# A four-layer convolution and attention network: sign convolutions with two weights packed in one float32r number, attention without a row-maximum pass

## The chip, the cores and the metric

The kernel runs on one core of a Trainium2 chip. The core has a matrix engine (TensorE, PE in the profile), a vector engine (DVE), a scalar engine (ACT), a general one (GpSimd, POOL) and a queue engine (SyncE, SP) that issues transfers. Each has its own program; they wait for each other through semaphores. TensorE writes to an accumulator memory (PSUM[...]) that DVE and ACT read. The metric is device time in microseconds (us), the median of several runs; the spans and times of single instructions come from a hardware profile of one execution, whose span is a few us longer.

## The reference, cut to what matters

The input is 16 images of 256 channels and 28 x 28 pixels. Each of the four layers keeps that shape.

```python
# layer 0: binary convolution, batch norm, residual
y  = conv3x3(sign(x), sign(w0)) * mean_abs(w0)
x1 = batchnorm(y) + x

# layer 1: sign convolution with float weights, two gated branches
res = prelu(x1, a_alpha1)
y = prelu(bn(conv3x3(sign(x1 + a_move), clip(a_w)), a_bn1), a_alpha2)
y = se_gate(s*x1 + (1-s)*y) * y * res          # gate: means, two small matrices, sigmoid
y = bn(y, a_bn2) + res
u = prelu(bn(conv1x1(sign(y + f_move), clip(f_w)), f_bn1), f_alpha2)
u = se_gate(s2*y + (1-s2)*u) * u
x2 = bn(u, f_bn2) + y

# layer 2: two binary convolutions; the batch norms use the batch's statistics
o = prelu(binconv(sign(batchnorm(x2)), w1), a1)
o = prelu(binconv(sign(batchnorm(o)), w2), a2)
x3 = prelu(batchnorm(o) + x2, a3)

# layer 3: attention over the 784 pixels of each image, 64 channels
q, k, v = Wq x3, Wk x3, Wv x3
out = Wp (softmax(q^T k / 8) v) + x3
```

A batch norm with the batch's own statistics needs all 16 images before any can go on, so there are barriers after layer 0, layer 1 and each convolution of layer 2.

## The kernel before

Channels lie on the 128 partitions (two halves), pixels on the free axis. Signs and sign weights are bfloat16. The float weights of layer 1 are split into three bfloat16 parts whose sum is exact, so each of its products is done three times.

```python
def conv3x3(ps, pad, wts, mo):          # called with [w0], w1 (three parts), [w2a], [w2b]
    n, last = 0, len(wts) * 18 - 1
    for w in wts:
        for k in range(2):
            for t in range(9):
                r, c = divmod(t, 3)
                for h in range(2):
                    T.matmul(               # line 145
                        ps[:, h, :HN].rearrange("p (a b) -> p a b", b=S),
                        lhsT=w[:, k, t, mo * P:(mo + 1) * P],
                        rhs=pad[:, k, r + h * HR:r + h * HR + HR, c:c + S],
                        start=(n == 0), stop=(n == last),
                    )
                n += 1
# ...
def conv2(b, w, alpha):                 # layer 2
    for mo in range(2):
        ps = conv_ps()                  # three tiles of two banks
        conv3x3(ps, pads[b % 2], [w], mo)
        p = prelu_n(ph, ps[:, :, :HN], alpha[:, mo:mo + 1])
        A.copy(halves(nt[b][:, mo, :]), ps[:, :, :HN])
        for h in range(2):
            V.bn_stats(stats[:, mo, 2 * b + h, :], p[:, h, :])
```

The attention computes the scores twice: once to find each row's maximum, and once, transposed, with the maximum subtracted through a 65th row of q and k.

```python
def row_max(b):
    # ...
    for c in range(NC_):                # 7 chunks of 112 rows
        ps = two_banks(pssc, "sc")
        for h in range(2):
            T.matmul(ps[:MC, h, :HN], lhsT=q[0:64, c * MC:(c + 1) * MC],
                     rhs=k_[0:64, h * HN:(h + 1) * HN], start=True, stop=True)      # line 543
        V.tensor_reduce(nm[:, c:c + 1], ps[:MC, :, :HN], AX.XY, ALU.max, negate=True)
# ...
def attend(b):
    # ...
    def scores(c):
        ps = two_banks(pssc, "sc")
        for h in range(2):
            T.matmul(ps[:MC, h, :HN], lhsT=k_[:, c * MC:(c + 1) * MC],
                     rhs=q[:, h * HN:(h + 1) * HN], start=True, stop=True)          # line 569
        es[c] = ph.tile([MC, 2, HN], F32, tag="es", name="es", bufs=3)
        A.activation(es[c], ps[:MC, :, :HN], AF.Exp, scale=0.125)
    # ...
            for h in range(2):
                T.matmul(av[:, h, :HN], lhsT=v_[:, c, :], rhs=es[c][:, h, :],
                         start=(c == 0), stop=(c == NC_ - 1))                       # line 581
    V.reciprocal(r, av[64:P, :, :HN])   # columns 64.. of v are ones: the denominators
    V.tensor_tensor(o, av[0:64, :, :HN], r, ALU.mult)
# ...
for b in range(B):
    nm = row_max(b)
    if pending is not None:
        project(*pending)
    if b + 1 < B:
        qkv(b + 1)
    put_max(b, nm)
    if b + 2 < B:
        finish2(b + 2)
    pending = (b, attend(b))
```

Here P = 128, N = 784, HN = 392 (half an image, one PSUM bank), HR = 14, S = 28, MC = 112, NC_ = 7. V, A, T are the vector, scalar and matrix engine. All 16 images' x2 and integers stay in SBUF.

Of the kernel before, what the change touches and what calls it, by code (L numbers as in the profile page):

```python
"""conv_seq d4 on 16x256x28x28: binary conv + BN, two-branch SE block, binary conv x2 + BN, attention.

Layout: channels on partitions (two halves of 128), pixels (784) on the free axis, one tile per
image.  Activations that are signs (-1, 0, 1) and sign weights are held in bfloat16, and
convolution sums of signs (integers of magnitude <= 2304) in int16: both hold them exactly.  The
float32 weights that meet sign activations (layer 1) are split into three bfloat16 parts whose sum
is the float32 weight, so that these products are exact too; everything else is float32.

Algebra used: stop_gradient(a - b) + b is a; sums of 2304 signs never reach the saturation of layer
0; the mean of s*x + (1-s)*y is taken from the two means; a per-channel constant of layer 1's output  # L10
is carried along (`cc`) into layer 2's last bias, as layer 2's first batch norm doesn't see it.
"""
# [10 lines left out]
BF = mybir.dt.bfloat16  # L23
I16 = mybir.dt.int16
AF = mybir.ActivationFunctionType
ALU = mybir.AluOpType
AX = mybir.AxisListType
PSUM = bass.MemoryType.PSUM

P = 128  # L30
B = 16
S = 28
N = S * S          # pixels of an image
HN = N // 2        # half an image: one matmul, one PSUM bank
HR = S // 2
K9 = 256 * 9
MC = 112           # attention rows per chunk
# [3 lines left out]
#: The per-channel vectors, in the order of their columns.  # L41
# [10 lines left out]
def conv_seq_kernel(ctx: ExitStack, tc: tile.TileContext, d: dict, out: bass.AP):  # L52
# [6 lines left out]
    xr = ctx.enter_context(tc.tile_pool(name="xr", bufs=B))  # L59

# [9 lines left out]

    pads = [const.tile([P, 2, S + 2, S + 2], BF, tag=f"pad{i}", name=f"pad{i}") for i in range(2)]
    for p in pads:
        nc.gpsimd.memset(p, 0.0)

# [7 lines left out]
    def inv_std(name, var):  # L82
        """1 / sqrt(var + EPS) of a [P, 2] tile, the square root's table corrected by a Newton step."""
# [9 lines left out]
    def affine(name, inv, gamma, beta, mean):  # L93
        """scale = gamma * inv and bias = beta - mean * scale."""
        s, c = vtile(name + "_s"), vtile(name + "_c")
        tt(s, gamma, inv, ALU.mult)
        tt(c, mean, s, ALU.mult)
        tt(c, beta, c, ALU.subtract)
        return s, c

# [1 line left out]
    def load_taps(pool, src, k, g):  # L102
        st = pool.tile([P, 3, 256], F32, tag="st", name="st", bufs=2)
# [3 lines left out]
    def sign_chunk(pool, dst, src, acc, k, g):  # L107
        """Three taps of sign(w) into dst, and their part of sum |w| in PSUM, [P, 2]."""
        st = load_taps(pool, src, k, g)
        A.activation(dst[:, k, 3 * g:3 * g + 3, :], st, AF.Sign)  # L110
        ab = pool.tile([P, 256], F32, tag="ab", name="ab", bufs=2)
        V.tensor_reduce(ab, st.rearrange("p t o -> p o t"), AX.X, ALU.add, apply_absolute_value=True)
        part = acc.tile([P, 2], F32, tag="sm", name="sumabs")
        for mo in range(2):
            T.matmul(part[:, mo:mo + 1], lhsT=ab[:, mo * P:(mo + 1) * P], rhs=ones, start=True, stop=True)
        return part

    def sign_weights(pool, dst, src, total, acc):
# [35 lines left out]
    def inner(pad, k):  # L154
        return pad[:, k, 1:S + 1, 1:S + 1]
# [517 lines left out]
```

## Time and profile before

The time is 2254.1 us, the median of three runs from 2253.57 to 2255.21. The profile's span is 2262.4 us.

| stretch of the span | us | PE busy | DVE busy | ACT busy | granted PE clock |
|---|---|---|---|---|---|
| opening, weights of layer 0 | 0 to 22.6 | 14.5 | 11.1 | 10.6 | 1.00 |
| layer 0 | 22.6 to 217 | 187.4 | 57.2 | 66.8 | 0.99 |
| layer 1 | 217 to 911 | 681.3 | 317.4 | 139.9 | 0.99 |
| layer 1's last images, barrier | 911 to 929 | 5.4 | 11.9 | 5.6 | 0.69 |
| layer 2, first convolution | 929 to 1131 | 199.4 | 100.7 | 61.4 | 0.98 |
| barrier | 1131 to 1143 | 0.9 | 9.6 | 2.3 | 0.73 |
| layer 2, second convolution | 1143 to 1345 | 198.2 | 139.4 | 57.9 | 0.99 |
| barrier, first images of attention | 1345 to 1490 | 124.0 | 90.9 | 29.9 | 0.66 |
| one image of attention | 1541 to 1592 | 47.5 | 36.9 | 12.1 | 0.80 |
| eight images of attention | 1648 to 2089 | 413.8 | 143.3 | 64.1 | 0.74 |
| the last of attention | 2089 to 2262 | 154.1 | 49.2 | 21.4 | 0.70 |

Busy times are sums over the instructions of an engine in the stretch. Matmuls are pipelined and their ends are modelled, so a busy PE need not work at its peak; the time from one start to the next is the better measure. The granted clock is the share of full speed that the hardware gave TensorE. A float32 matmul appears as two records, each with a weight load of its own. In a line of a group, the name after the engine is the operation, then output<-inputs, shapes, type and count; after the bar come the busy time in us and the mean of one in ns, and then the engine's idle time before the group and what ended it.

### The profile page before, as it was taken

How to read it: one execution, taken by the hardware profiler on the slowest of the kernel's cores; microseconds unless marked ns; L12 is line 12 of the kernel's file. 1: busy time of each engine (PE TensorE's matmuls, PEld its weight loads, DVE VectorE, ACT ScalarE, POOL GpSimd, SP SyncE). 2: the span in 40 equal slices, each digit the busy share in tenths (PEclk: the TensorE clock that was granted, in tenths of full speed). 3: DMA queues.
4: the chain of work that ended last, by engine and by line, in shares of the span. 5: the costliest groups of instructions: out<-in, count | busy, mean ns of one | idle time of the engine just before them, and what ended most of it. 6: DMA issues, size and time to landing. Idle time of an engine off the chain costs nothing.

```text
span 2262.4 us, 22710 instructions
## 1 busy us (share of the span) xinstructions
PE 2126.3 (94%) x9896; PEld 1170.4 (52%) x9896; DVE 1041.2 (46%) x1628; ACT 496.2 (22%) x659; POOL 6.5 (0%) x13
## 2 busy tenths in 40 slices
PE   8998999999999998699989979999999999999997
PEld 4554555555555555355545544444444444444443
DVE  5213244454454454554567765677653233222232
ACT  5322122122122111323222321222211111111111
POOL 0000000000000000000000000000000000000000
PEclk9999999999999999799999985688778777777776
DMA  5221000000000000100000000000000000000000
GB/s 204 73 72 43 1 29 29 15 29 15 15 29 15 15 15 1 42 1 1 1 1 1 1 5 1 14 14 15 14 14 15 14 15 14 14 14 14 15 15 28
DMA packets 11603, 50.11 MB, mean 22 GB/s; under 512 B 1776, under 2 KB 2160, under 8 KB 11504
## 3 DMA queue, kind: packets, MB, share of 16 engines
q1 hardware_dynamic: 11504, 48.67, 6.2%
q8 instruction: 77, 1.26, 0.2%
q14 instruction: 22, 0.18, 0.0%
HBM read 35.82 MB, written 12.85 MB: 22 GB/s over the span
## 4 chain that ended last, share of the span: by engine, by line
PE 90%; DVE 8%; ACT 1%; issue 0%; DMA 0%; SPq 0%; ACTq 0%
PE cv L145 53%; PE sc L543 10%; PE sc L569 7%; PE av L581 6%; PE mi L594 4%; DVE r L586 4%; PE cv L372 3%; PE mi L522 3%; PE mi L531 2%; PE av L554 2%; PE gate L343 1%; DVE nm L547 1%; DVE p L187 1%; DVE x L515 0%; DVE t L186 0%; DVE x L511 0%
## 5 line engine op out<-in xcount | busy, mean ns | idle before, releaser
L145 PE MATMUL cv<-pad,w 128*128 128x392 bf16 x4608 | 799.4, 333 | 8.7 <-ACT pad L305 8.7
L145 PEld LDWEIGHTS <-w 128*128 128x128 bf16 x4608 | 445.0, 97 | 343.6 <-issue 12.2
L543 PE MATMUL sc<-qk 64*112 64x392 f32 x448 | 263.8, 764 | 51.6 <-DVE nm L547 51.6
L543 PEld LDWEIGHTS sc<-qk 64*112 64x112 f32 x448 | 116.3, 267 | 186.9 <-issue 116.9
L145 PE MATMUL cv<-pad,w2b 128*128 128x392 bf16 x1152 | 198.3, 334 | 11.1 <-ACT pad L465 11.1
L569 PE MATMUL sc<-qk 65*112 65x392 f32 x448 | 202.8, 575 | 0.0
L145 PE MATMUL cv<-pad,w2a 128*128 128x392 bf16 x1152 | 198.3, 333 | 2.4 <-ACT pad L436 2.4
L294 DVE TENSOR_SCALAR t<-sy,vec 128x784 f32<-128x784 f32 x32 | 20.1, 628 | 340.7 <-ACT sy L318 340.7
L581 PE MATMUL av<-es,va 112*128 112x392 f32 x448 | 170.2, 509 | 1.6 <-ACT es L574 1.6
L586 DVE RECIPROCAL r<-av 64x784 f32<-64x784 f32 x16 | 80.9, 5057 | 190.3 <-PE av L581 190.3
L547 DVE TENSOR_REDUCE nm<-sc 112x1 f32<-112x784 f32 x112 | 108.9, 972 | 121.2 <-PE sc L543 120.8
L145 PEld LDWEIGHTS <-w2b 128*128 128x128 bf16 x1152 | 111.9, 97 | 97.5 <-issue 13.6
L145 PEld LDWEIGHTS <-w2a 128*128 128x128 bf16 x1152 | 112.2, 98 | 87.3 <-issue 3.9
L186 DVE TENSOR_SCALAR t<-cv,vec 128x784 f32<-128x784 f32 x64 | 66.2, 1034 | 158.6 <-PE cv L145 158.6
L574 ACT ACTIVATE es<-sc 112x784 f32<-112x784 f32 x112 | 91.9, 823 | 205.3 <-PE sc L569 205.2
L569 PEld LDWEIGHTS sc<-qk 65*112 65x112 f32 x448 | 85.7, 202 | 82.9 <-issue 71.5
L581 PEld LDWEIGHTS av<-es,va 112*128 112x128 f32 x448 | 87.7, 196 | 69.4 <-issue 18.7
L446 ACT CAST n<-cv 128x784 int16<-128x784 f32 x64 | 52.0, 812 | 229.3 <-DVE p L187 229.3
L318 ACT ACTIVATE sy<-cv,abn_c,abn_s 128x784 f32<-128x784 f32 x32 | 32.1, 1003 | 315.4 <-PE cv L145 315.4
L594 PE MATMUL mi<-o,wp 64*128 64x392 f32 x128 | 88.3, 831 | 7.2 <-DVE o L587 6.2
L246 DVE BATCH_NORM_STATS2 stats<-cv 128x6 f32<-128x392 f32 x64 | 33.4, 564 | 125.8 <-ACT y L244 125.7
L522 PE MATMUL mi<-x,wqk 128*128 128x392 f32 x128 | 68.0, 688 | 14.3 <-DVE x L515 14.3
(182 smaller groups left out, 1536.9 us busy)
## 6 DMA issues: line engine op xcount, KB each, us to landing
xs<-in_x_dram SPq DMA_DIRECT2D x32, 784.0 KB, 4.3
out_dram<-x SPq DMA_DIRECT2D x16, 784.0 KB, 3.3
st<-in_w_dram SPq DMA_DIRECT2D x12, 384.0 KB, 3.9
st<-in_w2a_dram SPq DMA_DIRECT2D x6, 384.0 KB, 3.1
st<-in_w2b_dram SPq DMA_DIRECT2D x6, 384.0 KB, 3.2
stf<-in_fw_dram SPq DMA_DIRECT2D x1, 256.0 KB, 2.8
wqk<-in_wqk_dram SPq DMA_DIRECT2D x1, 128.0 KB, 2.1
wv<-in_wv_dram SPq DMA_DIRECT2D x1, 64.0 KB, 1.9
```

Of the source, the lines that this page charges most:

```text
L145: T.matmul(ps[:, h, :HN].rearrange("p (a b) -> p a b", b=S), lhsT=w[:, k, t, mo * P:(mo + 1) * P], rhs=pad[:, k, r + h * HR:r + h * HR + H ...
L186: V.tensor_scalar(t, n, 0.0, alpha, ALU.min, ALU.mult)
L372: T.matmul(ps[:, h, :HN], lhsT=w[:, k, mo * P:(mo + 1) * P], rhs=z2[b][:, k, h * HN:(h + 1) * HN], start=(n == 0), stop=(n == 5),)
L446: A.copy(halves(nt[b][:, mo, :]), ps[:, :, :HN])
L522: T.matmul(ps[:, h, :HN], lhsT=wqk[:, k, :], rhs=x2[b][:, k, h * HN:(h + 1) * HN], start=(k == 0), stop=(k == 1),)
L543: T.matmul(ps[:MC, h, :HN], lhsT=q[0:64, c * MC:(c + 1) * MC], rhs=k_[0:64, h * HN:(h + 1) * HN], start=True, stop=True,)
L547: V.tensor_reduce(nm[:, c:c + 1], ps[:MC, :, :HN], AX.XY, ALU.max, negate=True)
L569: T.matmul(ps[:MC, h, :HN], lhsT=k_[:, c * MC:(c + 1) * MC], rhs=q[:, h * HN:(h + 1) * HN], start=True, stop=True,)
L574: A.activation(es[c], ps[:MC, :, :HN], AF.Exp, scale=0.125)
L581: T.matmul(av[:, h, :HN], lhsT=v_[:, c, :], rhs=es[c][:, h, :], start=(c == 0), stop=(c == NC_ - 1))
L586: V.reciprocal(r, av[64:P, :, :HN])
L594: T.matmul(ps[:, h, :HN], lhsT=wp[:, mo * P:(mo + 1) * P], rhs=o[:, h, :], start=True, stop=True)
```

## The change

**Sign convolutions.** A sum of at most 2304 signs is a small integer. The change puts the weights of two output channels into one float32r number, a + 4095 b (a for the first half of the channels, b for the second), and convolves once for both. ACT rounds the sum divided by 4095 to the integer part (adding and DVE then taking away 1.5 x 2^23), and two more matmuls with scaled unit matrices separate the halves: -4095 times the rounded value is added to the first half's sum, and the value itself goes to the second. To stay in range, only 15 of the 18 taps are packed; the last three are done for each half by itself.

```diff
+            sg = pool.tile([P, 3, 256], BF16, tag="t1", name="sg", bufs=2)
+            A.activation(sg, st, AF.Sign, saturate=False)
+            V.scalar_tensor_tensor(dst[0][:, n], sg[:, :, P:], PACK, sg[:, :, 0:P], ALU.mult, ALU.add)
 ...
+    def sign_conv(pss, pad, w, temp):
 ...
+        for h in range(2):
+            for n in range(5):
+                for t in range(3):
+                    product(pss[0], h, w[0][:, n, t, :], n, t, n + t == 0, n + t == 6)
+            r, bs[h] = temp("t1"), temp("up", FR)
+            A.activation(r, pss[0][:, h, :HN], AF.Identity, bias=rounding, scale=1.0 / PACK)
+            V.tensor_scalar(bs[h], r, -ROUND, None, ALU.add)
+        for h in range(2):
+            for mo in range(2):
+                for t in range(3):
+                    product(pss[mo], h, w[1][:, t, mo * P:(mo + 1) * P], 5, t, mo == 1 and t == 0, False, mo == 0)
+        for h in range(2):
+            for mo in range(2):
+                T.matmul(
+                    pss[mo][:, h, :HN], lhsT=unpack[mo], rhs=bs[h], start=False, stop=True,
+                    skip_group_check=(mo == 0),
+                )
```

**Layer 1.** The float weights are split into two float32r parts instead of three bfloat16 ones. Two output rows are computed from four combinations of the padded rows (a minimal-filtering transform: four products in place of six), which DVE forms in float32r. The parametric ReLU is done as x + (1 - alpha) * relu(-x), its ReLU on ACT. The two gates' small matmuls are joined. Integers and x2 go to DRAM and come back.

```diff
+            terms = (
+                (e0, e1, ALU.subtract), (o0, e1, ALU.add), (e1, o0, ALU.subtract), (o0, o1, ALU.subtract)
+            )
+            for pair in ((1, 2), (0, 3)):
+                for k in range(2) if b == 0 else (slice(0, 2),):
+                    for u in pair:
+                        x, y, op = terms[u]
+                        tt(vs[b % 2][:, u, k], x[:, k], y[:, k], op)
 ...
+        def conv(b, mo, u, ps):
+            n = 0
+            for k in range(2):
+                for w in w1:
+                    for c in range(3):
+                        T.matmul(
+                            ps.rearrange("p (a b) -> p a b", b=S),
+                            lhsT=w[:, k, c, u, mo * P:(mo + 1) * P],
+                            rhs=vs[b % 2][:, u, k, :, c:c + S],
+                            start=(n == 0), stop=(n == 11),
+                        )
+                        n += 1
 ...
+            A.activation(t1, ps[:, 0, :HN], AF.Identity, bias=c1[:, mo:mo + 1], scale=s1[:, mo:mo + 1])
+            V.scalar_tensor_tensor(up, ps[:, 1, :HN], s1[:, mo:mo + 1], t1, ALU.mult, ALU.add)
+            V.scalar_tensor_tensor(vp, ps[:, 1, :HN], ns1[:, mo:mo + 1], t1, ALU.mult, ALU.add)
 ...
+            nc.gpsimd.dma_start(out=x2d[b], in_=x2[b])
```

At the barriers a batch of matmuls on unused data is put on TensorE, to keep its clock from falling.

```diff
+        def keep_busy(v, n):
+            A.copy(idle[:, 0:2], v)
+            ps = pss.tile([P, 512], F32, tag="sm", name="unused")
+            for _ in range(n):
+                T.matmul(ps, lhsT=idle[:, 0:P], rhs=idle, start=True, stop=True)
```

**Attention.** The scores are not shifted by their row maximum. Queries of the two half images lie on partitions 0 to 63 and 64 to 127, so that the two score matmuls of a chunk use different rows of the array; the values and denominators of the two halves use different columns. The denominators are one matmul pair on a sum over chunks that POOL and DVE form. The residual is added by a transfer that accumulates into SBUF. The order of the instructions on PE, ACT, DVE and POOL is fixed by the program. A sum of the denominators and of their reciprocals is compared with 1e18 at the end; only if it is larger, an attention with shifted scores runs again behind a branch.

```diff
+    def finish_a(b, n=slice(0, N)):
+        for k in range(2):
+            v = x[b][:, k, n]
+            A.activation(v, v, AF.Identity, bias=bg3[:, k:k + 1], scale=sg3[:, k:k + 1])
+            if b < 3:
+                V.tensor_tensor(v, v, x2[b][:, k, n], ALU.add)
+        if b >= 3:
+            nc.gpsimd.dma_start(out=x[b], in_=x2d[b], accum_op=ALU.add)
 ...
+    def scores(b, c):
+        ps, k_ = two_banks(pssc, "sc"), ks[b].rearrange("p h n -> p (h n)")
+        for h in range(2):
+            rows = slice(64 * h, 64 * h + 64)
+            T.matmul(
+                ps[:MC, h, :HN], lhsT=k_[rows, c * MC:(c + 1) * MC], rhs=qs[b][rows], start=True, stop=True
+            )
+        e = es[b, c] = buf("es", 7, shape=(MC, 2, HN))
+        A.activation(e, ps[:MC, :, :HN], AF.Exp, scale=0.125)
 ...
+    def side_by_side(ps, w, e, start, stop):
+        for h in range(2):
+            T.matmul(ps[64 * h:64 * h + 64, :HN], lhsT=w, rhs=e[:, h, :], start=start, stop=stop)
 ...
+        for b in range(B):
 ...
+            scores(b, 1)
+            sum_up(b, 1)
+            scores(b, 2)
 ...
+            scores(b, 3)
+            sum_up(b, 2, 3)
 ...
+                queries_keys(b + 1)
+                project_v(b + 1)
 ...
+            scores(b, 4)
+            scores(b, 5)
 ...
+            for c in range(4):
+                values(b, c)
 ...
+                denominators(b - 1)
+                invert(b - 1)
+            scores(b, 6)
 ...
+                scores(b + 1, 0)
+            for c in range(4, NC_):
+                values(b, c)
```

## The prediction

> **What bounds the kernel now.** I read the page from its slices and its chain first, then cut the span at the stage boundaries that the chain shows, then took the price of each kind of instruction from the groups.
>
> In the slices of the page (40 of 56.6 us each), TensorE is busy almost everywhere; the third line is its granted clock:
>
> ```profile
> PE   8998999999999998699989979999999999999997
> ...
> PEclk9999999999999999799999985688778777777776
> ```
>
> The clock is full for the convolutions and falls to 0.5 to 0.8 in the attention, the last 16 slices. The chain that ended last says the same by line: L145 (every 3x3 convolution) 53%, and the attention's matmuls most of the rest:
>
> ```profile
> PE 90%; DVE 8%; ACT 1%; issue 0%; DMA 0%; SPq 0%; ACTq 0%
> PE cv L145 53%; PE sc L543 10%; PE sc L569 7%; PE av L581 6%; PE mi L594 4%; DVE r L586 4%; PE cv L372 3%; PE mi L522 3%; PE mi L531 2%; PE av L554 2%; PE gate L343 1%; DVE nm L547 1%; DVE p L187 1%; DVE x L515 0%; DVE t L186 0%; DVE x L511 0%
> ```
>
> Busy time by stretch (the columns are PE, weight loads, DVE, ACT, POOL, granted clock, DMA share, GB/s), for layer 0, layer 1, layer 2's second convolution and eight images of attention, and below them two short stretches of one attention image:
>
> ```profile
> 22.60:217.00 194.40, 187.42 (x1100) 106.41 (x1099) 57.22 (x109) 66.77 (x85) 0.00 (x0) 0.99 0.25 81
> 217.00:911.00 694.00, 681.34 (x4096) 392.49 (x4096) 317.36 (x699) 139.94 (x222) 0.00 (x0) 0.99 0.05 17
> 1143.00:1345.00 202.00, 198.16 (x1152) 111.73 (x1150) 139.41 (x190) 57.92 (x63) 1.52 (x4) 0.99 0.00 1
> 1648.00:2089.00 441.00, 413.83 (x1137) 214.58 (x1137) 143.29 (x123) 64.06 (x84) 0.00 (x0) 0.74 0.04 15
> ```
>
> ```profile
> 2090.00:2096.00 6.00, 6.00 (x10) 2.82 (x10) 2.61 (x3) 0.00 (x0) 0.00 (x0) 0.50 0.00 0
> 2130.00:2137.00 7.00, 7.00 (x23) 3.87 (x22) 0.00 (x0) 1.75 (x3) 0.00 (x0) 1.00 0.00 0
> ```
>
> So all stages are bound by TensorE. In attention it does 10 records in 6 us at clock 0.5 and 23 in 7 us at clock 1.0. The half clock begins with each image's idle gap of 3.3 to 3.7 us (TensorE waits for the row maxima, which queue behind a 5.06 us reciprocal) and lasts until about 2117 in this image that began at 2089.
>
> Price of one matmul, from the chain in order of time, where the engine never pauses:
>
> ```profile
> 971.13 12.29 PE cv L145 x72
> 341.72 18.43 PE cv L145 x108
> 380.26 3.98 PE cv L372 x24
> ```
>
> 12.29/72 = 170.7 ns for 392 columns of bf16 out of the padded image, and 3.98/24 = 165.8 ns out of a dense tile. Float32 at full clock: a chunk of two matmuls (four records) takes 1.32 us in the attention's timeline, 660 ns per matmul, four times as long.
>
> Prices on the other engines (mean ns is the number after the comma):
>
> ```profile
> L311 DVE SCALAR_TENSOR_TENSOR xs<-t,vec,xs 128x784 f32<-128x784 f32 x32 | 33.0, 1031 | 0.5
> L389 DVE BATCH_NORM_STATS2 stats_x<-x 128x6 f32<-128x392 f32 x64 | 31.4, 553 | 0.0
> L586 DVE RECIPROCAL r<-av 64x784 f32<-64x784 f32 x16 | 80.9, 5057 | 190.3 <-PE av L581 190.3
> L574 ACT ACTIVATE es<-sc 112x784 f32<-112x784 f32 x112 | 91.9, 823 | 205.3 <-PE sc L569 205.2
> ```
>
> **What the Trainium skill says.** "FP8 and Floating Point Precision", TensorE Precision Notes: true float32 takes four passes through the array; a reduced-precision float32 reads four bytes and truncates to a 22-bit format. The trace agrees with the four passes (660 against 165.8 ns). No run here shows float32r; that it is the one-pass form is my inference, supported by the pack factor 4095 (4095 +- 1 fits 12 bits). "TensorE: Matmul & The Clock Gate", Weight-path perf modes: the fast weight load is not for float32. The trace agrees: 96 ns for bf16 weights, 178 ns for float32 at full clock, yet 28 records of L531, each with its own 112-column load, pass in 2.83 us, 101 ns each, so a load hides under 165 ns of streaming. Same page, Part 1: an idle window of about 3.4 us halves the clock. The trace agrees on the fall, but shows it lasting some 28 us of busy work, longer than the page's one busy window. Same page, Part 3: matmuls on different row or column groups run at the same time, but start and end strictly in order. No matmul of before uses this.
>
> **The change part by part, per image (16 images).**
>
> *Sign convolutions (layer 0, layer 2 twice).* 72 bf16 matmuls become 2 x (15 packed + 6 plain + 2 unpack) = 46. At 170.7 ns, 12.29 becomes 7.85 us. Beside it ACT has in layer 2 two signs (2 x 1.04), two rounding halves (0.58 each by slope) and two ReLUs (0.81), 4.9 us; DVE two half-size subtractions (0.42), two 1.03 us combinations, four statistics (0.56), 5.1 us. Both fit under 7.85. The rounding chain (0.58 + 0.42 + hand-overs) lies under some ten matmuls that the program order puts before the unpack; I add 0.35 us per image for it when ACT is busy: 8.2 x 16 = 131 us for each of three convolutions, 394 in all. Before they took 194 + 202 + 202 = 598.
>
> *Layer 1.* The 3x3 convolution with three bf16 parts (216 matmuls) becomes a row-pair transform, four products over half the rows with two float32r parts: 2 x 4 x 12 = 96. The 1x1 goes from 24 to 16. (96 x 170.7 + 16 x 165.8) = 19.0 us, with the gates 20. But DVE now has: entry 2 x (1.03 + 0.08), transform 4 x 1.03 (840 elements), residual 2 x 1.03, eight half-size combinations out of PSUM at 0.62, four accumulating combinations 2 x 2 x 1.11, the product with the residual 2 x 1.11, branch two 2 x 1.03 + 4 x 0.55, four tiny ones: 2.2 + 4.1 + 2.1 + 5.0 + 4.5 + 2.2 + 4.3 + 0.6 = 25.0 us. With 40 instructions and the 0.03 us between back-to-back ones in the timeline: 26.2. ACT has about 16. So the bound moves from TensorE (42.7 us an image) to DVE; I add 1.3 us for waits in its order (gates come back through PE and ACT): 27.5 x 16 = 440, plus 12 to enter and 18 to drain the two images in flight: 470. Before: 712 from 217 to 929.
>
> *Attention.* The row-maximum pass (14 float32 matmuls, seven reductions), the transposition of the maxima and the two-stage wait on the reciprocal go. Left: scores 14, values 14, denominators 2, projection 4, all in pairs that can overlap, queries and keys 4, and v 28 records (2.83 us). Two float32 records per matmul at 330 ns, in order, one pair overlapping only where neighbours differ in row or column group: n consecutive pairs take 2n + 1 slots. Scores 3+2+2 pairs 17 slots, values 4+3 16, denominators 3, projection 6: 42 x 0.33 = 13.9, plus 2.64 and 2.83 = 19.4 us. With perfect overlap 16.7, with none 27.9. ACT: seven exponentials 5.8, two affine 2.1, two ReLUs 1.7, copies 2.8, two sums 1.0 = 13.4. DVE: three additions 2.9, reciprocal at half the columns 2.5, the rest 5.5 = 10.9. TensorE stays the bound, and with no gap over 3 us in the order the clock should stay at 1.0: 19.5 x 16 = 312. Before: 909 from 1353. The fallback with shifted scores sits behind a branch; the largest scaled score of these inputs, worked out from the reference, is 20, the denominators below 1e9, so it is not entered. The test of it and the last store I put at 6 us, the first and last image's chains at 20.
>
> *Moved to DRAM.* Integers, x2 and a copy of the finished x are written and read again, some 3 MB per attention image in 19 us, 160 GB/s. The opening of before moves 284 GB/s, so I count it hidden. The accumulating transfer has an iteration of slack.
>
> *Sum.* Opening 18 (all packed weights come before the convolutions); convolutions 394; layer 1 470; gaps between stages 8 + 8 + 9 (9.6 us of DVE work in the 12 us gap at 1131 before; batches of idle matmuls keep the clock); attention 338. Total 1245, and I say **1240 us**.
>
> **Rivals.** (1) *Float32r streams at two cycles a column.* Four-byte columns speak for it; against it, float32 itself already reads four bytes and I see only its passes. Then 46 x 0.33 = 15.2 us an image (+350 over three convolutions) and layer 1 becomes PE-bound at 38 (+170): about 1770. With four passes, about 3100, slower. (2) *Pairs of float32 matmuls don't overlap*: 27.9 instead of 19.4 an image, +136: 1380. (3) *Layer 1's order stalls DVE more*, say 32 us an image: +72, 1320. (4) *The clock halves in attention anyway*, because some wait passes 3.4 us: up to +200. (5) *Better overlap* and DVE without stalls: 16.7 and 26.2: about 1175.
>
> **Range and chances.** The middle of (2), (3) and (5) gives 1130 to 1400. One in ten is for rival (1), still faster by far; only four-pass float32r, or a stage that breaks down, loses. Faster 0.96, same 0.01, slower 0.03.
>
> **What would show it.** Groups of the packed convolution: 392 columns at about 170 ns start to start, 7.8 to 8.3 us an image; a period near 15 us is rival (1). Layer 1: period 27 to 28 us with DVE above 90% and TensorE near 75%; TensorE full instead would be a slower float32r. Attention: period near 19.5 us, PEclk 9 in its slices; 28 us is rival (2), a 5 in PEclk rival (4). If TensorE is not the bound in attention but waits on ACT, my ACT sum was too small.

## The result, and the profile after

The changed kernel takes 1233.4 us (median of four runs, 1230.0 to 1234.5) against 2254.7 us of the kernel before beside it (2253.6 to 2255.5): a ratio of 0.5467, with a 95% interval of 0.5459 to 0.5476. The profile below, of the execution that took 1230.0 us, has a span of 1228.1 us. The prediction was 1240 us.

The page of the changed kernel, slices (40 of 30.7 us each) and then the chain that ended last, by engine:

```profile
PE   5999989999999999984987997999979999999995
...
PEclk9999999999999999995998998999989999999997
...
PE 74%; DVE 12%; ACT 10%; issue 2%; DMA 1%; POOL 1%; SPq 0%; ACTq 0%; POOLq 0%; DVEq 0%
```

The low clock of the attention is gone: the attention's slices, the last ten, are 9 but for the very last. TensorE has 74% of the chain instead of 90%; DVE and ACT, which before carried 9% together, carry 22%.

Busy time by stretch of the changed kernel: layer 0, layer 1's steady part, layer 2's first and second convolution, the attention's steady part; then one image of layer 1 and one of the attention (columns: PE, weight loads, DVE, ACT, POOL, granted clock, DMA share, GB/s):

```profile
20.20:166.00 145.80, 145.01 (x730) 136.83 (x731) 64.19 (x148) 76.30 (x119) 8.79 (x15) 1.00 0.42 149
179.70:553.00 373.30, 357.17 (x1922) 347.19 (x1923) 339.71 (x627) 235.16 (x349) 16.00 (x28) 0.99 0.21 74
580.00:743.00 163.00, 149.51 (x748) 138.76 (x747) 77.52 (x142) 76.06 (x101) 0.00 (x0) 0.97 0.27 94
758.00:903.00 145.00, 144.88 (x730) 134.58 (x730) 67.99 (x122) 70.91 (x94) 0.00 (x0) 0.99 0.00 1
924.00:1194.00 270.00, 264.67 (x1542) 139.54 (x1544) 151.47 (x143) 184.12 (x290) 96.69 (x58) 1.00 0.44 123
384.90:408.30 23.40, 22.38 (x121) 21.69 (x121) 21.83 (x41) 14.82 (x24) 0.53 (x1) 1.00 0.25 86
1053.00:1071.20 18.20, 17.93 (x107) 9.45 (x105) 10.64 (x10) 12.57 (x20) 6.64 (x5) 1.00 0.48 134
```

Layer 0 and the second convolution of layer 2 are full of TensorE. In the first convolution the same 16 images take 163 us, with 13 us of idle TensorE. In layer 1 PE and DVE are both over 90% busy (96 and 91%), so the row alone doesn't say which one sets the pace; TensorE near 75% was the prediction's sign there, and it failed. In the attention TensorE is full, at full clock, with ACT and DVE well below it.

Beside the terms of the prediction (gaps counted with the stage that follows, except where named):

| stretch | predicted us | profile us | difference |
|---|---|---|---|
| opening | 18 | 20.2 | +2 |
| layer 0 | 131 | 145.8 | +15 |
| layer 1 with entry, drain and the gap after it | 478 | 414 | -64 |
| layer 2, first convolution | 131 | 163 | +32 |
| gap | 8 | 15 | +7 |
| layer 2, second convolution | 131 | 145 | +14 |
| gap and attention | 347 | 325 | -22 |
| sum | 1244 | 1228 | -16 |

So the total hit by luck: large errors of opposite sign cancelled. The experiments are about these errors, and about what carries the gain.

### The profile page after: what moved, and what is told of

Its sections match the earlier page's. It is cut to its first block, busy times and chain, and to the rows that moved or that the text cites. A ratio compares the mean times of both kernels' runs of the same rounds, so it can differ in the third digit from the quotient of the medians. Undisturbed runs are those within 1.5% of the kernel's fastest.

```text
span 1228.1 us, 15404 instructions
## 1 busy us (share of the span) xinstructions
PE 1125.3 (92%) x5940; PEld 934.6 (76%) x5944; DVE 784.3 (64%) x1405; ACT 691.5 (56%) x1047; POOL 140.9 (11%) x131
## 4 chain that ended last, share of the span: by engine, by line
PE 74%; DVE 12%; ACT 10%; issue 2%; DMA 1%; POOL 1%; SPq 0%; ACTq 0%; POOLq 0%; DVEq 0%
PE cv L198 32%; PE cv L468 15%; PE av L898 6%; PE sc L877 5%; PE mi L862 4%; PE sm L935 3%; PE cv L218 2%; DVE x L597 1%; ACT y L543 1%; DVE x L552 1%; ACT junk L929 1%; DVE stats L599 1%; ACT rn L428 1%; PE cv L565 1%; DVE xs L460 1%
## 5 line engine op out<-in xcount | busy, mean ns | idle before, releaser
L468 PE MATMUL cv<-vs,w 128*128 128x392 f32 x1536 | 301.7, 355 | 8.3 <-DVE y L501 7.2
L198 PE MATMUL cv<-fpad,wpk 128*128 128x392 f32 x1440 | 302.3, 358 | 0.8 <-DVE wpk L159 0.8
L468 PEld LDWEIGHTS cv<-vs,w 128*128 128x128 f32 x1536 | 286.2, 190 | 12.7 <-DVE y L501 9.9
L198 PEld LDWEIGHTS cv<-fpad,wpk 128*128 128x128 f32 x1440 | 271.8, 192 | 11.5 <-ACT t L210 7.7
L198 PE MATMUL cv<-fpad,wpl 128*128 128x392 f32 x576 | 138.5, 368 | 13.7 <-DVE p L711 9.7
L198 PEld LDWEIGHTS cv<-fpad,wpl 128*128 128x128 f32 x576 | 105.2, 194 | 32.2 <-ACT t L210 17.4
L711 DVE SCALAR_TENSOR_TENSOR p<-r,r,cv 128x784 f32<-128x784 f32 (+1 forms) x66 | 63.6, 1002 | 86.2 <-ACT r L710 86.2
L877 PE MATMUL sc<-q,k 64*112 64x392 f32 x448 | 90.1, 515 | 6.0 <-ACT es L881 4.4
L898 PE MATMUL av<-es,va 112*64 112x392 f32 x448 | 80.8, 499 | 0.0
L111 DVE TENSOR_TENSOR vs<-pad 128x840 fp32r<-128x840 bf16 (+1 forms) x68 | 64.1, 974 | 0.0
L710 ACT ACTIVATE r<-cv 128x784 f32<-128x784 f32 (+1 forms) x66 | 49.1, 790 | 10.2 <-PE cv L218 7.7
```

Of the source, the lines that this page charges most:

```text
L111: V.tensor_tensor(o, a, b, op)
L198: T.matmul(ps[:, h, :HN].rearrange("p (a b) -> p a b", b=S), lhsT=lhsT, rhs=pad[:, k, r + h * HR:r + h * HR + HR, c:c + S], start=start, s ...
L468: T.matmul(ps.rearrange("p (a b) -> p a b", b=S), lhsT=w[:, k, c, u, mo * P:(mo + 1) * P], rhs=vs[b % 2][:, u, k, :, c:c + S], start=(n == 0),
L711: V.scalar_tensor_tensor(p[:, h], r[:, h], beta[:, mo:mo + 1], ps[:, h, :HN], ALU.mult, ALU.add)
L877: T.matmul(ps[:MC, h, :HN], lhsT=k_[rows, c * MC:(c + 1) * MC], rhs=qs[b][rows], start=True, stop=True)
L898: T.matmul(ps[64 * h:64 * h + 64, :HN], lhsT=w, rhs=e[:, h, :], start=start, stop=stop)
```

## The experiments

"After" is the changed kernel. A run that was timed once is held against after's profiled execution, 1230.0 us; a run that was timed four times against after's median, 1233.4 us. Where a run leaves work out, its time is not that of a kernel that computes the reference.

### Is a float32r matmul slower than a bf16 one?

The sign convolutions of layer 2 run at 9.07 us an image where nothing holds them, and those of layer 0 at 9.0 on average: 7.85 were predicted for the matmuls, 8.2 with the rounding. The chain of the changed kernel, in order of time, in layer 2's second convolution (start, us, what):

```profile
777.59 6.83 PE cv L198 x35
...
786.66 6.82 PE cv L198 x35
```

6.83 / 35 = 195 ns for a 392-column matmul, but there are stalls in it. The timeline of the same stage (start, us, instructions; in brackets the idle time before them and what ended it):

```profile
804.62 2.81 PE L198 MATMUL cv<-fpad,wpk 128*128 128x392 f32 x14
...
807.26 0.92 PE L198 MATMUL cv<-fpad,wpl 128*128 128x392 f32 x4
...
808.10 2.76 PEld L198 LDWEIGHTS cv<-fpad,wpk 128*128 128x128 f32 x15 [0.27 <-ACT t L210]
...
811.89 1.06 PEld L198 LDWEIGHTS cv<-fpad,wpl 128*128 128x128 f32 x6 [0.27 <-ACT t L210]
```

From the first start to the next group 14 matmuls take 2.64 us, 189 ns each. Twice an image the weight load then waits for ACT's rounding, which reads the accumulator. At each of these places two starts in a row are some 285 ns apart instead of 190: 0.38 us an image in all. So 9.07 is 42 x 0.190 + 4 x 0.180 (the unit-matrix products) + 0.38.

The run replaces layer 2's padded images and sign weights by bfloat16; only the four matmuls with unit matrices stay float32r. Bfloat16 can't hold a + 4095 b, so the sums are not the layer's; the number of matmuls and columns is the same.

```diff
-    w2a = [packed_weights(wpool, tag="wa"), None]
+    w2a = [packed_weights(wpool, BF16, tag="wa"), None]       # the same for w2b and the plain weights
-    pads2 = float_pads(ph, "fpad")
+    pads2 = [ph.tile([P, 2, S + 2, S + 2], BF16, ...) for i in range(2)]
```

> Layer 2's padded signs and sign weights are bfloat16 instead of float32r (the packed numbers lose their low bits, so the sums are not the reference's); the same 46 matmuls an image, of which the 4 unpacking ones stay float32r. Theory F (a float32r matmul of 392 columns costs some 24 ns more than a bfloat16 one): an undisturbed image of layer 2 falls from 9.07 us to 42 x 170.7 + 4 x 180 = 7.9 us, the whole by some 35 us. Rival C (the period is set by the rounding chain through ACT and DVE): it stays within 0.2 us of 9.07.

1201.9 us. The chain and then the timeline of this run in the same stage:

```profile
770.86 6.12 PE cv L198 x35
...
779.02 6.12 PE cv L198 x35
```

```profile
773.93 2.71 PE L198 MATMUL cv<-fpad,wpk 128*128 128x392 bf16 x15
776.47 0.51 PE L198 MATMUL cv<-fpad,wpl 128*128 128x392 bf16 x2
```

The image falls from 9.07 to 8.17 us, 0.90 us or 21 ns for each of the 42 matmuls of an image that changed type. Twice 16 images give 29 us, and the whole fell by 28 (profiled runs). Fifteen packed matmuls in a row take 2.54 us from first start to the next group, 169 ns each, against 189. The means of all starts of the stage, with the gaps over 260 ns left out, say the same: 170 and 190 ns. So float32r does cost what the prediction missed: some 19 ns over bfloat16 in the same rows. Of the stalls 0.3 us an image remain.

### Weight load, strided rows, start address, or a fixed cost?

Four causes could stand behind those 19 ns. The weight load: the group row of the changed kernel has a mean of 192 ns for it (99 ns for bfloat16 in the run above), close to the 190 ns from start to start.

```profile
L198 PEld LDWEIGHTS cv<-fpad,wpk 128*128 128x128 f32 x1440 | 271.8, 192 | 11.5 <-ACT t L210 7.7 <-issue 1.2 <-ACT fpad L689 0.8
```

Or the rows: a matmul reads 28 of every 30 elements. Or a fixed cost per matmul. Or the address at which a read starts. The first run shortens the load in the first convolution (96 of the 128 weight columns in 36 of the 46 matmuls, so a quarter of the output channels is left out) and makes the read consecutive in the second (392 elements in a row, so other pixels than the convolution's).

```diff
-    T.matmul(ps[:, h, :HN]..., lhsT=lhsT, rhs=pad[:, k, r + h * HR:r + h * HR + HR, c:c + S], ...)
+    T.matmul(ps[0:m, h, :HN]..., lhsT=lhsT[:, 0:m], ...)                      # first: m = 96
+    T.matmul(ps[0:m, h, :HN], ..., rhs=flat(pad[:, k])[:, at:at + HN], ...)   # second: consecutive
```

> First convolution of layer 2: 36 of 46 matmuls use 96 of the 128 weight columns (a quarter of the output channels is left out of them). Second convolution: the moving columns are 392 consecutive elements instead of 14 rows of 28 out of rows of 30 (the taps' shifts are then not right). Theory L (the load of the weights sets the float32r period): an undisturbed image of the first falls from 9.07 to about 8.1 to 8.3 us, the second stays at 9.07. Theory S (reading short rows of 4-byte elements sets it): the first stays at 9.07, the second falls to about 46 x 0.179 = 8.2 us.

1225.0 us. Its chain, first in the convolution with 96 columns, then in the one with consecutive reads:

```profile
730.88 6.81 PE cv L207 x35
...
777.45 6.51 PE cv L201 x35
```

With 96 columns 35 matmuls take what they took with 128. With consecutive reads they take 0.32 us less (9 ns each), and the image 8.70 us instead of 9.07, not the 8.2 of theory S: the mean from start to start is 180 ns.

The second run takes 64 columns in the first convolution, and both cuts together in the second.

```diff
-    conv2(i, order[i], w2a, r1, cols=96)
+    conv2(i, order[i], w2a, r1, cols=64)
-    conv2(b, b, w2b, r2, dense=True)
+    conv2(b, b, w2b, r2, cols=96, dense=True)
```

> First convolution of layer 2: 36 of 46 matmuls use 64 weight columns (half of the output channels left out of them). Second convolution: 96 columns and consecutive moving elements together. Theory L: the first falls to 8.1 us or below, down to the streaming time of some 170 ns a matmul, and the second is no faster than 96 columns alone. Theory S: the first stays at 9.07; the second is as consecutive elements alone, about 8.2. If both add up, the second comes near 46 x 0.166 = 7.7 us.

1223.8 us; 9.00 us an image with 64 columns, 8.66 with both. The group row of this run shows that the load itself was shortened, from 192 to 140 ns:

```profile
L207 PEld LDWEIGHTS cv<-fpad,wpk 128*64 128x64 f32 x416 | 58.0, 140 | 20.7
```

A load that is 52 ns shorter leaves the mean from start to start at 190 ns, so the theory that the load sets the step falls, although its mean looks just like it. The rows hold half of the excess, about 10 of 19 ns.

The third run halves the streamed columns in the first convolution (64 weight columns by 196 pixels, so half the channels and half the pixels are left out) and starts every consecutive read in the second at element 0, 32, 128 or 256 (again other pixels).

```diff
+    m, hr = (64, HR // 2) if part else (P, HR)
+    T.matmul(ps[0:m, h, :hr * S]..., lhsT=lhsT[:, 0:m], rhs=pad[:, k, r + h * HR:r + h * HR + hr, c:c + S], ...)
+    at = (0, 32, 128, 256)[(n + t) % 4]
```

> First convolution of layer 2: 36 of 46 matmuls stream 196 columns instead of 392 (half of the pixels are left out of them), with 64 weight columns. Second: consecutive elements, all starting at a multiple of 32 elements (the taps' shifts are left out). Theory X (a float32r matmul has a fixed cost of some 13 to 26 ns over bfloat16): start to start of the 196-column ones inside a run is 82 + 26 = 108 ns, against 95 ns if the cost is per column. Theory A (starts off a 16-byte or larger boundary cost the rest of the difference between 189 ns in the run with consecutive elements and 179 ns in the 1x1 convolution): an image of the second falls from 8.70 to about 8.25 us; if not, it stays at 8.70.

1202.2 us. The timeline of TensorE in this run, first in the convolution with half columns, then in the one with aligned reads:

```profile
695.82 1.82 PE L208 MATMUL cv<-fpad,wpk 128*128 128x392 f32 x15
697.48 0.54 PE L208 MATMUL cv<-fpad,wpl 128*128 128x392 f32 x3
```

```profile
773.02 2.65 PE L200 MATMUL cv<-fpad,wpk 128*128 128x392 f32 x14
775.56 0.98 PE L200 MATMUL cv<-fpad,wpl 128*128 128x392 f32 x4
```

Thirteen 196-column matmuls and two whole ones (the row is named by its first) pass in 1.66 us: (1.66 - 2 x 0.19) / 13 = 98 ns, near half of 190. So the price goes by columns; at most some 4 ns are fixed per instruction. The aligned reads take 2.54 us for 14, 181 ns each, as the unaligned consecutive ones did, and the image is 8.68 instead of 8.70 us: the start address is worth next to nothing.

So of the 19 ns over bfloat16 in the same rows 10 are the rows and the start is nothing. Consecutive float32r reads, at 180 ns, are still 14 ns above the 166 of consecutive bfloat16 ones in the kernel before (3.98 / 24); what makes these 14 stays open. The 1x1 convolution of layer 1, which reads consecutive elements too, has 179 ns between starts (16 starts from 404.2 to 406.9 us), the same price.

### Does DVE set the pace of layer 1?

Layer 1's period is 23.4 us, with 96 + 16 float32r matmuls and PE busy for 22.4. If PE is the bound, half its matmuls must shorten the period. The run leaves out the lower float32r part of the 3x3 weights: 48 matmuls instead of 96, an output of lower precision.

```diff
-                for w in w1:
+                for w in w1[:1]:
-                            start=(n == 0), stop=(n == 11),
+                            start=(n == 0), stop=(n == 5),
```

> The 3x3 convolution of layer 1 uses only the upper float32r part of its weights (the lower part is left out): 48 matmuls an image instead of 96, nothing else changed. Theory V (VectorE is the bound of layer 1): the period of 23.4 us an image stays above 22.5, TensorE goes idle for some 9 us of it. Rival P (TensorE is the bound, it is busy 22.4 of 23.4 us): the period falls by several us, to 18 or less.

1226.8 us, some 3 us less. Layer 1's steady stretch in this run:

```profile
179.70:553.00 373.30, 272.24 (x1156) 250.38 (x1156) 341.27 (x630) 239.39 (x355) 15.96 (x28) 0.80 0.21 74
```

In the same 373.3 us DVE does as much as before (341 us), and PE, with 766 instructions fewer, has 101 us idle and a clock of 0.80. A lower clock stretches what is left, so the busy time falls by less than half; but TensorE, with a quarter of its time free, isn't the bound by its amount of work. What DVE waits for can be read in the two DVE timelines, first the changed kernel's and then this run's:

```profile
396.19 0.16 DVE L111 TENSOR_TENSOR gates<-gates,s 128x4 f32<-128x4 f32 x1 [1.52 <-ACT gates L535]
```

```profile
395.23 0.16 DVE L111 TENSOR_TENSOR gates<-gates,s 128x4 f32<-128x4 f32 x1 [3.50 <-ACT gates L535]
```

In these two images DVE's wait for the gates, which pass through PE and ACT, is 1.52 and 3.50 us. The mean period of 13 images is 23.4 us in the changed kernel and 23.7 in this run, so it doesn't follow the number of matmuls.

That doesn't make DVE's amount of work the bound. The chain of the changed kernel in one period:

```profile
384.88 8.97 PE cv L468 x46
...
395.44 0.73 ACT gates L535 x4
...
397.47 2.00 DVE x L552 x4
```

It is a loop: TensorE's matmuls up to the gates, ACT's gates and product, DVE's products, and then the next image's matmuls, which wait for DVE. Of its 23.4 us TensorE has 10.5, DVE 10.2 and ACT 1.8. DVE's row transform isn't on it; it lies beside TensorE's part, where DVE waits in the end. And this run took its matmuls mostly from behind the gates: ahead of them stand 37 to 48 a period, as against 48 to 52 in the changed kernel, and in the image shown 43 of them take 10.94 us, with the lower clock:

```profile
381.95 10.94 PE cv L468 x43
```

So the run leaves open whether the loop or DVE's sum of 21.8 us sets the period; in the changed kernel they are within 1.6 us of each other.

Why 21.8 us and not the 25 of the prediction shows in the changed kernel's DVE timeline:

```profile
397.47 1.03 DVE L552 SCALAR_TENSOR_TENSOR x<-xs,l_c,y 128x784 f32<-128x784 f32 x1
398.43 0.08 DVE L552 DVE_READ_ACCUMULATOR x<-xs,l_c,y 128x1 f32 x1
398.43 1.04 DVE L552 SCALAR_TENSOR_TENSOR x<-xs,l_c,y 128x784 f32<-128x784 f32 x1
```

An instruction of 1.03 us is followed by the next one after 0.96 us, and the accumulator read of 0.08 us takes no time of its own: the second product starts at the same 398.43. A sum of forty durations counts each overlap twice. The Trainium skill, "VectorE: DVE Perf Modes", The DRAIN you can't avoid, says that an instruction waits until the pipe has emptied, and that one that isn't held starts earlier; the trace agrees with the second half, 0.96 us from start to start for a duration of 1.03.

### Can DVE's share be given to the idle engine?

POOL is 1 to 4% busy in layer 1. The run gives it half of the row transform (two of the four combinations, from the second image on).

```diff
-                        tt(vs[b % 2][:, u, k], x[:, k], y[:, k], op)
+                        (nc.gpsimd if u in (0, 3) and b > 0 else V).tensor_tensor(vs[b % 2][:, u, k], x[:, k], y[:, k], op)
```

> Two of the four row combinations of layer 1 (those that TensorE needs last) are formed by GpSimd, for all images but the first. Theory V (DVE is the bound of layer 1, TensorE close behind at some 22): the period falls from 23.4 by 0.7 to 1.3 us, the whole by 10 to 20 us. Rival G (the wait for the gates sets the period, not DVE's amount of work): it falls by less than 0.3 us.

1249.2 us (1246.9 to 1252.7), ratio 0.5535 [0.5499, 0.557]: 16 us more than after, which neither expectation had. The timelines of POOL and of DVE in this run:

```profile
417.75 1.66 POOL L453 TENSOR_TENSOR vs<-pad 128x840 fp32r<-128x840 bf16 x1 [18.74 <-PE cv L468]
```

```profile
418.12 2.12 DVE L597 SCALAR_TENSOR_TENSOR x<-u,gates,x 128x784 f32<-128x784 f32 x1
...
434.16 0.63 DVE L501 SCALAR_TENSOR_TENSOR y<-cv,abn_s,up 128x392 f32<-128x392 f32 x1 [1.95 <-PE cv L468]
```

A product that takes 1.03 us alone takes 2.12 beside POOL. POOL's next instruction, from 421.13 to 422.80 us, runs beside DVE instructions that have one of their inputs in the accumulator memory, and these take 0.61 us as ever. The Trainium skill, "GPSIMD Engine Reference", Specifications, says that POOL shares its interfaces to SBUF, the on-chip memory, with VectorE and contends with instructions of two SBUF inputs, of which this is one; the trace agrees. The loss lies mainly in five earlier images, whose periods are 25.2 to 26.6 us. In four of them POOL's two instructions come one after the other, and the chain has two slow products, each 0.95 us in the changed kernel's chain:

```profile
316.03 2.40 DVE x L597
318.43 2.35 DVE xs L460
```

So the edit took work from DVE that was not on the chain and stretched work that was. In the later images, where one product is slowed, DVE is busy for 21.1 us, 0.7 less than in the changed kernel, and yet the period is 23.8 instead of 23.4: DVE waits more, here 1.95 us for PE. That speaks for the loop and against DVE's amount of work. It isn't shown by itself, since the order of the instructions came out differently too.

### Attention: do the pairs overlap?

The prediction let only neighbouring pairs overlap (2n + 1 slots of 0.33 us for n pairs). The changed kernel's chain in one image: four pairs of values, two pairs of scores (16 and 8 records):

```profile
1060.81 2.78 PE av L898 x16
...
1064.25 1.50 PE sc L877 x8
```

That is 0.70 and 0.75 us a pair, where two matmuls one after the other take 1.32. The run lets both score matmuls of a chunk use partitions 0 to 63 (both halves then use the first half's queries).

```diff
-            rows = slice(64 * h, 64 * h + 64)
+            rows = slice(0, 64)
```

> The two score matmuls of a chunk both use partitions 0 to 63 (the queries of the second half image are left out, those of the first are used twice); nothing else changes. Theory O (float32 matmuls on different row groups overlap almost fully, which is why a pair takes some 0.70 us in the profile and an image 18.1): each of the seven pairs goes to 1.32 us, an image to 22 to 22.5 us, the whole up by 62 to 70 us. Rival N (the pair is short for another reason, its overlap is not real): the image stays within 0.5 us of 18.1.

1296.0 us, 66 more than the profiled run of after. Its chain, again for two score pairs:

```profile
1011.62 2.81 PE sc L877 x8
```

1.41 us a pair instead of 0.75: 0.66 x 7 chunks = 4.6 us an image, and the image goes from 18.1 to 22.2 us. Sixteen times 4.1 is 66. The pairs of scores overlap nearly whole. For the values, on column groups, this was not tried; their 0.70 us a pair, where two matmuls in turn would take 1.32, says the same.

### Attention: the residual, the order, the clock

The residual by DVE for all images, without the accumulating transfer (x2 is loaded three images ahead):

```diff
-            if b < 3:
-                V.tensor_tensor(v, v, x2[b][:, k, n], ALU.add)
-        if b >= 3:
-            nc.gpsimd.dma_start(out=x[b], in_=x2d[b], accum_op=ALU.add)
+            V.tensor_tensor(v, v, x2[b][:, k, n], ALU.add)
```

> The residual of attention is loaded and added by VectorE (two additions of 0.97 us an image) in place of the accumulating transfer. Theory H (TensorE bounds attention, DVE has room: 10.6 of 18.2 us): within 5 us of 1233. Rival D (DVE's fixed order delays what TensorE waits for): the two additions show in full, 13 x 1.9 = 25 us longer.

1238.4 us (1237.5 to 1240.0), ratio 0.5485 [0.547, 0.55]. The accumulating transfer is worth about 5 us, which alone would be near the scatter; but the image goes from 18.1 to 18.8 us all through the stage. DVE goes from 10.6 to 12.3 us an image, so of its 1.7 us one us lies beside TensorE's work and 0.7 shows.

The attention's instructions ordered by the scheduler instead of by the program:

```diff
-    with tc.manual_schedule(engines={ET.PE, ET.Activation, ET.DVE, ET.Pool}):
+    if True:
```

> The attention's program order is not fixed; the scheduler orders the instructions of each engine. Theory M (the fixed order keeps TensorE fed): an image takes 19.5 us or more, the whole is 20 us or more longer. Rival N (TensorE has 17.9 us of work in any order): within 6 us of 1233.

1280.9 us (1280.5 to 1281.1), ratio 0.567 [0.5656, 0.5685]: 47 us more. The waits of this run from 924 to 1045 us (engine line <- releaser: us, times, longest):

```profile
POOL p L838 <- ACT p L834: 56.0, 11, 12.5
POOL sum L889 <- ACT es L881: 38.5, 3, 20.1
ACT rl L844 <- DMA p<-x2d: 30.7, 10, 8.8
...
PE av L898 <- ACT es L881: 19.4, 4, 7.2
```

The first four steps from image to image take 21.4, 26.4, 29.2 and 31.9 us, 109 in all, where the changed kernel takes 67; the later ones take 18.7 us, where it takes 18.1. So 42 of the 47 us are lost at the start of the stage, and the expected 19.5 us an image was not the reason. In this run's program on POOL four accumulating transfers stand between the sums of one image and those of the next, as long as there are any; in the changed kernel it is one. Read as a chain: POOL waits for ACT's affine pass before each transfer; ACT stands before a ReLU that needs one; exponentials queue behind that; and TensorE waits for exponentials. In the changed kernel TensorE waits 4.1 us for them in the whole steady stretch. That the place of the transfers is the cause is read from these waits; no run moved them alone.

The batches of idle matmuls at the barriers left out:

```diff
         def keep_busy(v, n):
-            A.copy(idle[:, 0:2], v)
-            ...
+            return
```

> The batches of matmuls on unused data at the four barriers are left out. Theory K (they keep the clock): after each barrier the granted clock is 0.5 for at least 3.4 us, up to some 28 us as in the attention of before, so each stage loses 2 to 14 us: 8 to 56 us in all. Rival N (the clock recovers at once): within 4 us of 1233.

1236.0 us (1234.5 to 1237.9), ratio 0.5475 [0.5459, 0.549]: the interval overlaps that of after. The clock does fall. This run, right after the barrier of layer 0:

```profile
179.00:183.00 4.00, 4.00 (x13) 4.00 (x14) 4.00 (x8) 1.09 (x2) 0.00 (x0) 0.50 0.01 3
183.00:187.00 4.00, 4.00 (x20) 3.98 (x19) 3.36 (x7) 0.94 (x2) 0.00 (x0) 0.84 0.00 0
```

In the changed kernel both stretches have 1.00, though after the next two barriers its first 4 us have 0.80 and 0.62. But in this run the clock is back at 184.3 us, 5.5 us after the first convolution matmul, and after the other three barriers it takes 4.1 to 6.1 us from the first large matmul. Over four barriers the time lost is about 2.6 us (medians), which can't be told from none. The idle matmuls keep the clock after this barrier, and there is little for them to save.

### What held up layer 2's first convolution

This stage computes as much as the second convolution and takes 18 us longer. The waits of ACT in it, in the changed kernel:

```profile
ACT sg L158 <- DMA st<-in_w2b_dram: 20.0, 5, 4.1
```

While it convolves, the kernel loads and signs the second convolution's weights. Their staging tiles come from a ring of three, named "r", which holds the ReLU results of the convolution as well. A load can't begin before a tile is free, and the sign that needs it stands in ACT's program ahead of the rounding that TensorE waits for. One held image of the changed kernel, in its chain:

```profile
618.26 1.05 ACT fpad L689
...
619.33 0.32 SPq L272
...
619.74 4.95 DMA st<-in_w2b_dram
...
624.71 1.05 DVE ab L169
```

ACT's pass over the padded image frees the buffer of an x2 load; SyncE issues that load and, behind it in its program, the weights' load, which is on the chain for 4.95 us. From there the chain goes through DVE's sum of the absolute weights and a matmul that adds it up; ACT's sign and rounding, which wait for the same transfer, end at about the same time (626.1 us). Five images of 13.2 to 13.9 us instead of 9.07, less 2.3 us in the image after them, are the whole excess of 20 us. The run gives the staging two tiles of its own:

```diff
-    steps = [rest[1]] + both(*sign_weights(ph, w2b, d["w2b"], sf2, pss, ("r", 3)))
+    steps = [rest[1]] + both(*sign_weights(ph, w2b, d["w2b"], sf2, pss, ("st2", 2)))
```

> The second convolution's weights are staged in two buffers of their own, in place of the three that they share with the ReLU results of layer 2. Theory W (five images of the first convolution of layer 2 take 13.2 instead of 9.1 us because ACT waits in order for a weight load whose buffer comes free late, and TensorE waits for ACT's rounding): those images fall to 9.1 to 9.5 us, the whole to 1213 to 1217 us. Rival B (ACT's and DVE's extra work for the weights, some 2 us an image each, is what holds TensorE): they stay above 11 us, the gain is under 10 us.

1213.1 us (1212.8 to 1215.2), ratio 0.5373 [0.534, 0.5405]. It computes all that the reference asks, and is 20 us shorter than after: the best of the kernels here that leave nothing out. The wait is gone from ACT's list, and the chain shows the same stage without a break:

```profile
620.90 6.83 PE cv L198 x35
...
629.97 6.83 PE cv L198 x35
```

Only the ring was changed. Whether the missing tile or its place behind the x2 load in SyncE's program held the load is not separated: with the new tiles the load also stands further ahead, 8.2 us before its sign (619.65 and 627.87 us) where it was 5.0.

The last run joins this edit to that of the transform on POOL, both as shown.

> Both together. The two stages are apart in time, so the gains should add: 1195 to 1205 us, if the two single runs give what theories W and V say.

1234.5 us (1233.0 to 1235.5), ratio 0.5463 [0.543, 0.5496]: 21 us above the staging edit alone, where POOL's transform cost 16 alone. The effects add to within some 5 us; the expected 1195 to 1205 was not reached, since one of them is a loss.

## Why the prediction was right, and where not

**What bounds each stage.** Right: TensorE in the convolutions and the attention, with the clock at 1.0. In layer 1 right in so far as TensorE's amount of work no longer bounds (the run with half the matmuls left the stage's length as it was); that DVE's does is not shown, and the chain there is a loop through TensorE, ACT and DVE. The DRAM traffic stayed hidden: the attention moves 123 GB/s, where 160 were estimated, and TensorE is full.

**"At 170.7 ns, 12.29 becomes 7.85 us."** This step failed in its size. The count of 46 was right; the price, taken from bfloat16, is 190 ns in float32r (180 for the four unit-matrix products), so the matmuls are 8.7 us an image. Of the 19 ns the runs place 10 in the rows of 28 out of 30. The 0.35 us put on for the rounding was right in size: 0.38 us of stalls, in which the next weight load waits for ACT's rounding. Sum over three convolutions: some 43 us too little. Rival (1), two cycles a column, would have been 330 ns; the truth lay an eighth of the way there.

**The first convolution's weights.** Not in the prediction at all: "all packed weights come before the convolutions" was said of the opening, and the second set of weights, which comes during a convolution, was left out of account. 18 to 20 us, shown by the staging edit.

**"25.0 us. With 40 instructions and the 0.03 us between back-to-back ones in the timeline: 26.2."** The list of DVE's work was right, and the 0.03 us had the wrong sign: neighbouring instructions overlap by some 0.08 us instead of standing 0.03 apart. Measured, the 40 take 21.8 us and the wait for the gates 1.5 (1.3 were allowed): 23.4 instead of 27.5, 16 x 4.1 = 66 us too much. TensorE's own work there was put at 20 us and is 22.4, mostly by the float32r price.

**"n consecutive pairs take 2n + 1 slots."** Failed: 0.66 to 0.75 us a pair at any n, close to the perfect overlap of 0.66 that the text named as its other end. Seven score, seven value, one denominator and two projection pairs take 12.1 us instead of 13.9; with 0.5 us of waits the image is 18.1 instead of 19.4. Rival (2), no overlap, was tried for the scores alone and made +66.

**Rivals (3) and (4).** Neither came. In the image of layer 1 shown DVE waits once, 1.5 us; the clock in the attention's steady part is 1.00. ACT's sum, 13.4 predicted, is 12.6 and hidden.

**The gaps.** 15 and 21 us where 8 and 9 stood, together 19 us too little. They were not taken apart.

The range held the result with room, but the 7 us by which the estimate missed are not its precision: +61 us in the convolutions, -64 in layer 1 and -22 in the last gap and the attention are.

## What to carry to other kernels

Price an instruction of a new type by measuring it, and take starts and not durations when a long row of instructions on one engine is summed: the two mistakes made here were 11% of a matmul and 8% of a DVE instruction, and each cost some 40 us or more. Take out the stalls before a mean is called a price, and give each stall its cause. When a stage loads for the next one while it computes, give the staging its own tiles; with a ring shared with results the transfer got onto the chain here. An idle engine isn't free help when it reads the memory that the busy one reads; and before work is taken off a busy engine, see whether that work is on the chain.

## What the runs showed of the hardware that was not expected

- From start to start a float32r matmul of 392 columns takes 190 ns out of padded rows and 180 out of consecutive elements; bfloat16 takes 170 and 166. The price goes by columns (98 ns for 196), and not by the weight load, which takes 192, 167 or 140 ns for 128, 96 or 64 columns and hides.
- Float32 pairs on row groups or column groups take 0.66 to 0.75 us; the scores' pairs, put on one row group, take 1.41.
- After an idle barrier TensorE had its full clock back 4 to 6 us after the next stage's first large matmuls, while in the attention of before, with float32 matmuls mostly on 64 or 65 rows, the half clock lasted 20 to 31 us an image. What makes the difference was not tried.
- A DVE instruction with two SBUF inputs took 2.1 to 2.5 us instead of 1.03 while POOL ran an elementwise instruction of its own; two with one input in the accumulator memory kept their 0.61 us.
